# One more in-place DMA addition ahead of the third layer of a bias network

## The chip, the cores and the metric

The kernel runs on one core of one Trainium2 chip. The metric is the device time in microseconds (us) of one execution. In what follows PE is the matmul engine (TensorE), PEld its weight loads, DVE VectorE, ACT ScalarE, POOL GpSimd and SP SyncE, which here only issues DMAs.

## The reference

Four layers follow each other on an input of 2 x 512 x 32 x 32 floats. Only the first matters here, an attention whose keys are sampled at learned offsets and whose bias is a small network. For each of 8 groups of channels and each of 2 images (16 heads of the reference; the kernel handles two at a time, hence 8 pairs that it also calls groups, of 64 keys each):

```python
pos = grid_q[:, :, None, :] - grid_kv[:, None, :, :]       # 1024 queries x 64 keys x 2
bias = jnp.sign(pos) * jnp.log1p(jnp.abs(pos))
bias = jax.nn.relu(bias @ cpb_w1 + cpb_b1)                 # first layer: 128 hidden units
bias = jax.nn.relu(bias @ cpb_w2 + cpb_b2)                 # second layer: 128 hidden units
bias = (bias @ cpb_w3 + cpb_b3)                            # third layer: one number
sim = jnp.einsum('bhid,bhjd->bhij', qh, kh) + bias
attn = jax.nn.softmax(sim, axis=-1)
```

After it come a multilayer perceptron with a residual, a linear attention, a second attention and a gated output, all of which this change leaves as they are.

## The kernel before

All of it is one program in float32. The attention stage is one long loop over 512 keys (8 groups of 64), taken as 256 pairs `p` of keys. For each key the first layer is one DVE instruction, `first` (L353): it adds a row of `tab` for the key's column to one for its row and clips below at zero, and writes a tile `h` of 128 hidden units x 2048 (queries of two heads). `tab` is loaded by SP for 8 keys at a time (L161) and scaled by ACT (L173). There are 4 buffers for `h`.

The second layer, `second` (L619), takes the pair's two `h` tiles through a 128 x 128 weight matrix in four parts `o` of 32 output units. Each part is 8 matmuls of 128 x 32 by 512 columns, which go to the four column groups of the PE array (the trace has two records for each matmul, 16 for a part). ACT evicts each part with the bias and the Relu (L628) into tiles `r0` to `r3`; `hid` gives them 5, 1, 3 and 1 buffers. So the 32 partitions of one column group hold 32 hidden units of one (half of the queries, head), and four column groups are one tile.

The third layer is a weighted sum over the 128 hidden units. The weights' signs and sizes are folded into the second layer beforehand (`counted`, `placed`, `spread_out`), so that most of this sum is additions, of tiles and of neighbouring partitions:

- `combine` (L634, DVE) adds part 1 to part 0 and part 3 to part 2, with a ratio `rel`.
- `join` (L637) adds `r2` to `r0` by an accumulating DMA on POOL's queue, 512 KB.
- `fold` (L642) adds the odd partitions of `r0` to the even ones, an accumulating DMA on POOL's queue, 256 KB.
- `shift` (L649) copies every fourth partition to every fourth of a tile `xs`, on SP's queue, 128 KB; `d` shifts it, so that four pairs fill one `xs`.
- `meet` (L653) adds the other half of the folded partitions to it, on POOL's queue, 128 KB, and ends the life of `r0`.
- `third` (L664, PE) takes two `xs` tiles with 4 matmuls against the 33-column constant `cw3` into a PSUM tile `psim`; two such steps, with the constant shifted by a column, accumulate one `psim` of 32 keys.

What goes where in time is written out by hand. `at(n, when, fn, ...)` puts a call into a list for key `n` and for the even (0) or odd (1) parts of the second layer at that key; `run` calls them in that order, and `pin` keeps each engine's instructions in program order. So each engine, and each of the DMA queues of POOL and SP, works its list off in order, and an instruction that waits holds up all behind it on its engine. In the loop, `join(p - 1)` comes at key 2p, after part 1. The other transfers are given their keys by:

```python
at(2 * p + 4, 0, fold, p)
at(2 * p + 6, 0, shift, p)
at(2 * p + 7, 0, meet, p)
```

Beside the pairs run three plans of small steps, each placed by the same lists. `prepare(g)` samples a group's values and makes its keys and values (L685 to L760; `keys` and `values` write `kblk` and `vblk`, `weighted` by the output weights `wo` into `vwo`). `attend(g)` evicts `psim` (L791), transposes it onto the scores (`flip`, L803 and L816), and does the softmax (`top` L831, `sub` L835, `exp` L845, `total` L849, `inverse` L852, `norm` L856, `back` L862, `keep_` L871). `chain` computes the sampling offsets of the later groups (its taps are L230 on DVE), spread over keys 4 to 86 for groups 2 and 3 and 97 to 213 for groups 4 to 7.

After the loop the remaining transfers, the last third step and the last `attend` follow, without `pin`; beside them the scheduler places the output projection, 64 matmuls `po` (L1040), and the loads and sums of the first weights of the perceptron (L990, L1003, L973 to L983).

Of the kernel before, what the change touches and what calls it, by code (L numbers as in the profile page):

```python
# [10 lines left out]
F32 = mybir.dt.float32  # L11
AF = mybir.ActivationFunctionType
ALU = mybir.AluOpType
# [3 lines left out]
P = 128  # L17
B, C, H, W = 2, 512, 32, 32
# [39 lines left out]

_ORDER = [("same", P), ("below", P), ("place", P), ("rank", 1), ("third", 33)]
_CAT, _n = {}, 0  # L60
# [12 lines left out]
def conv_seq(  # L73
# [61 lines left out]
    with ExitStack() as ctx_l0:  # L135
# [11 lines left out]

        vwo = l0.tile([P, KC * B, C], F32, name="vwo")
        nc.gpsimd.memset(kblk, 0.0)
# [37 lines left out]
        def pin(ins):  # L187
            return tc.keep_in_program_order(ins) if started else ins
# [150 lines left out]
        sb3 = l0.tile([P, 4, 2], F32, name="sb3")  # L339
        cw3 = l0.tile([P, 33], F32, name="cw3")  # L340
        rel = l0.tile([P, 2], F32, name="rel")
# [23 lines left out]
        with tc.tile_pool(name="a", bufs=1) as a, tc.tile_pool(name="aps", bufs=3, space=PSUM) as aps, tc.tile_pool(  # L365
# [96 lines left out]
            def counted():  # L462
                pin(ve.tensor_copy(od[:, 7:9], pcnt))
                pin(ve.tensor_scalar(cpbw, cpbw, maj, None, ALU.mult))


                pin(ve.tensor_scalar(maj, total, 8.0, None, ALU.is_ge))
                pin(ve.tensor_scalar(t0, maj, -1.0, 1.0, ALU.mult, ALU.add))
                pin(ve.tensor_scalar(t1, total, -1.0, 16.0, ALU.mult, ALU.add))
                pin(ve.scalar_tensor_tensor(t0, t1, t0, below, ALU.mult, ALU.add))  # L470
                pin(ve.tensor_tensor(t1, oc("rank"), below, ALU.subtract))
                pin(ve.scalar_tensor_tensor(neg, total, maj, t1, ALU.mult, ALU.add))
                pin(ve.tensor_tensor(t0, t0, neg, ALU.subtract))
                pin(ve.scalar_tensor_tensor(t1, t0, pos, neg, ALU.mult, ALU.add))
                pin(ve.scalar_tensor_tensor(perm, oc("place"), t1, oc("same"), ALU.is_equal, ALU.mult))
# [119 lines left out]


        with tc.tile_pool(name="hid", bufs=3) as hid, tc.tile_pool(name="sm", bufs=1) as sm, tc.tile_pool(name="hps", bufs=2, space=PSUM) as hps, tc.tile_pool(
            name="sps", bufs=1, space=PSUM
# [13 lines left out]
            def second(p, o):  # L612

                ph = hps.tile([P, 2, 512], F32, name="ph")
                for i in range(2):
                    for t in range(4):
# [9 lines left out]
                        )  # L626
                r = hid.tile([P, 2, 512], F32, name=f"r{o}", bufs=(5, 1, 3, 1)[o])
                pin(nc.scalar.activation(r, ph, AF.Relu, bias=sb3[:, o, 1:2]))  # L628
# [9 lines left out]

            def fold(p):

                r = rs[p, 0]
                pin(nc.gpsimd.dma_start(r[0::2], r[1::2], accum_op=ALU.add))  # L642

            def shift(p):

                t, d = divmod(p, 4)
                if d == 0:
                    xs_[t] = hid.tile([P, 2, 512], F32, name="xs", bufs=3)
                pin(nc.sync.dma_start(xs_[t][d::4], rs[p, 0][0::4]))  # L649

            def meet(p):
                t, d = divmod(p, 4)
                pin(nc.gpsimd.dma_start(xs_[t][d::4], rs.pop((p, 0))[2::4], accum_op=ALU.add))  # L653

            def third(g, u):
                kb, i = divmod(u, 2)
                if i == 0:
                    psims[g, kb] = sps.tile([P, 512], F32, name=f"psim{kb}")
                for a in range(2):
                    xs = xs_.pop(g * J // 8 + 2 * u + a)  # L660
                    for c in range(2):
                        m = 2 * c + a
                        pin(
                            nc.tensor.matmul(  # L664
                                psims[g, kb][m * 32 : (m + 1) * 32, :],
                                lhsT=cw3[:, 1 - i : 33 - i],
                                rhs=xs[:, c, :],
                                start=(i == 0),
                                stop=(i == 1),
                                skip_group_check=True,  # L670
                            )
                        )

            def prepare(g):

                k, b = divmod(g, B)
                st = {}
                n = J * (g - 1) + 32
                here = slice(CO_AT[k] * P + b * J, CO_AT[k] * P + (b + 1) * J)
# [50 lines left out]
                def ordered(to, of):  # L730

                    to, of = to.rearrange("p (c x i) -> p c x i", c=2, i=2), of.rearrange("p (i x c) -> p c x i", c=2, i=2)
                    return to, of

                def keys():
                    for h, kb in np.ndindex(2, 2):
                        hs, ks = slice(h * DH, (h + 1) * DH), slice(kb * 32, (kb + 1) * 32)
                        to, of = ordered(kblk[hs, g % 2, h, ks], st["pk"][hs, 0, ks])
                        pin(nc.scalar.activation(to, of, AF.Identity, scale=DH**-0.5))

                def values():
                    for h, kb in np.ndindex(2, 2):
                        hs, ks = slice(h * DH, (h + 1) * DH), slice(kb * 32, (kb + 1) * 32)
                        to, of = ordered(vblk[hs, g % 2, h, ks], st["pk"][hs, 1, ks])
                        pin(nc.vector.tensor_copy(to, of))
# [13 lines left out]
                def weights():  # L759
                    pin(nc.scalar.copy(vwo[:, g, :], st["pw"]))  # L760

# [140 lines left out]
            for g in range(NG):  # L902
                prepare(g)
                for u in range(4):
                    at(J * g + 16 * u + 24, 0, third, g, u)
                if g < NG - 1:
                    attend(g, J * (g + 1) + 9, True)
            for p in range(NK // 2):
                at(2 * p + 4, 0, fold, p)
                at(2 * p + 6, 0, shift, p)  # L910
                at(2 * p + 7, 0, meet, p)

# [15 lines left out]

            chain(1, 2, 86, 82)
            chain(2, 4, 213, 116)  # L930

# [103 lines left out]
        for t in range(NT // 512):  # L1035
            ts_ = slice(t * 512, (t + 1) * 512)
            for o in range(KC):
                po = mh.tile([P, 512], F32, name="po")
                for k in range(KC):
                    nc.tensor.matmul(  # L1040
                        po,
                        lhsT=vwo[:, k * B + t // 2, o * P : (o + 1) * P],
                        rhs=q[:, k, ts_],
                        start=(k == 0),
                        stop=(k == KC - 1),
                    )
# [838 lines left out]
def _layout(a):  # L1885
# [50 lines left out]

    rank = p // 32 * 4 + p % 4
    same = p[:, None] % 32 // 4 == p[None] % 32 // 4
    put("same", same.astype(f), order)
    put("below", (same & (rank[:, None] < rank[None])).astype(f), order)  # L1940
    put("place", (np.array([0, 2, 1, 3])[p // 32] * 4 + p % 4).astype(f)[None], order)
    put("rank", rank.astype(f)[:, None], order)

    put("third", (np.arange(33)[None] == (1 + 8 * (p // 32) + 2 * (p % 4))[:, None]).astype(f), order)
    put("npy", -(4 * np.arange(8)[None] + p[:, None] // 32).astype(f))
# [56 lines left out]
```

## Time and profile before

| what | us |
|---|---|
| median of 3 runs (2698.12 to 2698.23) | 2698.2 |
| the profiled execution | 2697.67 |
| its span, from the first to the last instruction | 2695.9 |
| PE busy in the span | 2653.6 (98%) |
| DVE busy in the span | 2251.3 (84%) |
| ACT busy in the span | 1538.4 (57%) |
| POOL busy in the span | 669.8 (25%) |
| attention stage, first to last second-layer matmul | 44.0 to 1900.5 |

The page describes one execution. It gives, for each group of like instructions, the line and engine, what is written and read, the shape and the count; then, after the bar, the busy time in us and the mean ns of one; then the engine's idle time just before them and what ended it. Busy times of single instructions overlap at their ends: the trace has 2291 ns for a `first`, while the next instruction on DVE starts 2200 ns after it. So sums of durations are a little too long, and starts are used where it matters.

### The profile page before, as it was taken

How to read it: one execution, taken by the hardware profiler on the slowest of the kernel's cores; microseconds unless marked ns; L12 is line 12 of the kernel's file. 1: busy time of each engine (PE TensorE's matmuls, PEld its weight loads, DVE VectorE, ACT ScalarE, POOL GpSimd, SP SyncE). 2: the span in 40 equal slices, each digit the busy share in tenths (PEclk: the TensorE clock that was granted, in tenths of full speed). 3: DMA queues.
4: the chain of work that ended last, by engine and by line, in shares of the span. 5: the costliest groups of instructions: out<-in, count | busy, mean ns of one | idle time of the engine just before them, and what ended most of it. 6: DMA issues, size and time to landing. Idle time of an engine off the chain costs nothing.

```text
span 2695.9 us, 48423 instructions
## 1 busy us (share of the span) xinstructions
PE 2653.6 (98%) x19574; PEld 967.3 (36%) x19574; DVE 2251.3 (84%) x2009; ACT 1538.4 (57%) x1920; POOL 669.8 (25%) x784
## 2 busy tenths in 40 slices
PE   8999999999999999999999999999999999999997
PEld 4223323232332323333333333333444444455544
DVE  6999999999999999999999999999554445525646
ACT  7676677777667777866877776776221111001334
POOL 0333333333333333333333333333100000000001
PEclk9999999999999999999999999999999999999998
DMA  4777877877777787787788788787400000100001
GB/s 129 165 165 162 168 158 161 169 157 162 163 166 158 165 170 157 165 168 161 162 195 173 154 179 188 163 174 159 94 30 24 16 24 24 62 17 1 1 0 63
DMA packets 109327, 335.04 MB, mean 124 GB/s; under 512 B 18576, under 2 KB 28304, under 8 KB 108336
## 3 DMA queue, kind: packets, MB, share of 16 engines
q0 software_dynamic: 69632, 234.93, 46.7%
q1 hardware_dynamic: 38896, 96.51, 10.4%
q8 instruction: 154, 2.52, 0.4%
q14 instruction: 69, 0.57, 0.1%
q10 hardware_dynamic: 576, 0.51, 0.1%
HBM read 58.99 MB, written 4.46 MB: 24 GB/s over the span
## 4 chain that ended last, share of the span: by engine, by line
PE 81%; DVE 9%; issue 6%; ACT 2%; DMA 1%; POOL 1%; DVEq 0%; ACTq 0%; POOLq 0%
PE ph L619 51%; DVE h L353 4%; PE A L1105 4%; PE D L1105 4%; PE C L1105 4%; DVE r L634 3%; PE B L1105 2%; PE po L1040 2%; PE pg L1248 1%; PE pa L1359 1%; PE pu L1282 1%; PE psim L664 1%; PE pscore L1491 1%; DMA xs<-r 1%; PE pt L1511 1%
## 5 line engine op out<-in xcount | busy, mean ns | idle before, releaser
L619 PE MATMUL ph<-h,w2a 128*32 128x512 f32 x16384 | 1779.1, 593 | 6.0 <-ACT r L628 3.3
L628 ACT ACTIVATE r<-ph,sb 128x1024 f32<-128x1024 f32 x1024 | 1141.1, 1114 | 510.5 <-PE ph L619 487.3
L353 DVE CUSTOM_DVE_ANT_1 h<-tab 128x2048 f32<-128x2048 f32 x512 | 1172.9, 2291 | 13.0 <-PE ph L619 10.0
L619 PEld LDWEIGHTS ph<-h,w2a 128*32 128x32 f32 x16384 | 520.2, 109 | 1226.6 <-issue 801.7
L634 DVE SCALAR_TENSOR_TENSOR r<-r,rel,r 128x1024 f32<-128x1024 f32 x512 | 658.0, 1285 | 16.4 <-ACT r L628 15.8
L642 POOL DMA_DIRECT2D r<-r x256 | 219.5, 857 | 961.2 <-DMA r<-r 936.1
L637 POOL DMA_DIRECT2D r<-r x256 | 245.2, 958 | 280.4 <-DVE r L634 243.6
L653 POOL DMA_DIRECT2D xs<-r x256 | 306.6, 1198 | 12.2 <-issue 6.1
L173 ACT ACTIVATE tab<-tab,vec 128x256 f32<-128x256 f32 x252 | 136.9, 543 | 0.0
L1293 POOL MEMSET M<- 128x512 f32 x2 | 1.0, 524 | 435.3 <-DVE x L1169 435.3
L1145 ACT COPY u<-A 128x512 f32<-128x512 f32 x16 | 9.4, 585 | 146.9 <-PE A L1105 146.9
L1776 POOL TENSOR_TENSOR x<-x,aff 128x512 f32<-128x512 f32 x7 | 7.0, 1031 | 329.0 <-ACT e L1741 329.0
L1124 ACT ACTIVATE h<-h,vec 128x512 f32<-128x512 f32 x32 | 23.1, 721 | 113.7 <-DVE h L1127 113.7
L1127 DVE TENSOR_TENSOR h<-C,u 128x512 f32<-128x512 f32 x32 | 22.1, 691 | 48.2 <-PE C L1105 47.9
L1105 PE MATMUL A<-xn,w 128*128 128x512 f32 x128 | 60.3, 593 | 0.8 <-DVE x L1047 0.8
L1105 PE MATMUL C<-hT,w 128*128 128x512 f32 x128 | 60.3, 592 | 0.0
L1105 PE MATMUL A<-h,w 128*128 128x512 f32 x128 | 60.1, 592 | 0.0
L1040 PE MATMUL po<-q,vwo 128*128 128x512 f32 x128 | 56.3, 594 | 0.0
L230 DVE SCALAR_TENSOR_TENSOR acc<-q,vec,acc 128x128 f32<-128x128 f32 (+3 forms) x88 | 46.2, 525 | 0.8
L1165 DVE TENSOR_TENSOR x<-D,x 128x512 f32<-128x512 f32 x32 | 22.1, 691 | 25.8 <-PE D L1105 25.7
L856 ACT ACTIVATE e<-e,den 128x64 f32<-128x64 f32 x128 | 41.8, 338 | 1.9 <-DVE den L852 1.9
L1165 DVE TENSOR_TENSOR x<-C,x 128x512 f32<-128x512 f32 x32 | 22.1, 690 | 24.8 <-PE C L1105 24.8
(365 smaller groups left out, 1867.6 us busy)
## 6 DMA issues: line engine op xcount, KB each, us to landing
r<-r POOLq DMA_DIRECT2D x256, 512.0 KB, 5.2
r<-r POOLq DMA_DIRECT2D x256, 256.0 KB, 3.4
xs<-r SPq DMA_DIRECT2D x256, 128.0 KB, 3.9
xs<-r POOLq DMA_DIRECT2D x256, 128.0 KB, 5.6
tab<-fd SPq DMA_DIRECT2D x63, 512.0 KB, 5.6
lw<-in_l_w_dram SPq DMA_DIRECT2D x5, 1024.0 KB, 9.0
x<-in_x_dram SPq DMA_DIRECT2D x4, 1024.0 KB, 10.5
w<-in_mlp_w_dram SPq DMA_DIRECT2D x8, 512.0 KB, 4.3
```

Source lines behind the costliest of these rows:

```text
L173: return nc.scalar.activation(tf, tf if src is None else src[:, :, ax, :], AF.Identity, bias=0.0 if ax == 0 else v("L0_conv_cpb_b1"), scal ...
L230: pin(nc.vector.scalar_tensor_tensor(dst, src, wt_, dst, ALU.mult, ALU.add))
L353: nc.vector._custom_dve(TENSOR_ADD_SAT, out=h1, in0=columns.unsqueeze(1).to_broadcast([P, 32, 2, 32]), in1=rows_.unsqueeze(3).to_broadcast ...
L619: nc.tensor.matmul(ph[t * 32 : (t + 1) * 32, i, :], lhsT=w2a[:, o], rhs=h1s[2 * p + i][:, half * 16 : (half + 1) * 16, h, :], start=True, ...
L628: pin(nc.scalar.activation(r, ph, AF.Relu, bias=sb3[:, o, 1:2]))
L634: pin(nc.vector.scalar_tensor_tensor(r0, r1, rel[:, i : i + 1], r0, ALU.mult, ALU.add))
L637: pin(nc.gpsimd.dma_start(rs[p, 0], rs.pop((p, 2)), accum_op=ALU.add))
L642: pin(nc.gpsimd.dma_start(r[0::2], r[1::2], accum_op=ALU.add))
L653: pin(nc.gpsimd.dma_start(xs_[t][d::4], rs.pop((p, 0))[2::4], accum_op=ALU.add))
L1040: nc.tensor.matmul(po, lhsT=vwo[:, k * B + t // 2, o * P : (o + 1) * P], rhs=q[:, k, ts_], start=(k == 0), stop=(k == KC - 1),)
L1105: nc.tensor.matmul(banks[bank], lhsT=a[an][k], rhs=b_[bn_][k], start=(i < 4 and k == 0), stop=(k == n - 1), skip_group_check=True,)
L1165: nc.vector.tensor_tensor(to, t, to, ALU.add)
```

## The change

The partitions of the second layer are placed so that 8 neighbours, not 4, belong to one sum. A second `fold` with a stride of 2 adds every fourth partition's neighbour (64 partitions become 32, 128 KB), so `shift` and `meet` move 16 partitions (64 KB each) and 8 pairs fill one `xs`. A `psim` of 32 keys then needs one third step of 4 matmuls with a 32-column constant, and no accumulation. There are 8 third-layer matmuls per group where there were 16. `r0` gets 7 buffers. `vwo` is halved: the values of the second image are written over `wo`. `keys` and `values` become one instruction per head. The plans of `prepare`, `attend` and `chain` come 4 keys later. The core of the diff:

```diff
-        vwo = l0.tile([P, KC * B, C], F32, name="vwo")
+        vwo = l0.tile([P, KC, C], F32, name="vwo")
...
-                pin(ve.tensor_scalar(maj, total, 8.0, None, ALU.is_ge))
+                pin(ve.tensor_scalar(maj, total, 16.0, None, ALU.is_ge))
...
-                r = hid.tile([P, 2, 512], F32, name=f"r{o}", bufs=(5, 1, 3, 1)[o])
+                r = hid.tile([P, 2, 512], F32, name=f"r{o}", bufs=(7, 1, 3, 1)[o])
...
-            def fold(p):
+            def fold(p, step):
 
                 r = rs[p, 0]
-                pin(nc.gpsimd.dma_start(r[0::2], r[1::2], accum_op=ALU.add))
+                pin(nc.gpsimd.dma_start(r[0 :: 2 * step], r[step :: 2 * step], accum_op=ALU.add))
 
             def shift(p):
 
-                t, d = divmod(p, 4)
+                t, d = divmod(p, 8)
                 if d == 0:
                     xs_[t] = hid.tile([P, 2, 512], F32, name="xs", bufs=3)
-                pin(nc.sync.dma_start(xs_[t][d::4], rs[p, 0][0::4]))
+                pin(nc.sync.dma_start(xs_[t][d::8], rs[p, 0][0::8]))
 
             def meet(p):
-                t, d = divmod(p, 4)
-                pin(nc.gpsimd.dma_start(xs_[t][d::4], rs.pop((p, 0))[2::4], accum_op=ALU.add))
+                t, d = divmod(p, 8)
+                pin(nc.gpsimd.dma_start(xs_[t][d::8], rs.pop((p, 0))[4::8], accum_op=ALU.add))
...
-            def third(g, u):
-                kb, i = divmod(u, 2)
-                if i == 0:
-                    psims[g, kb] = sps.tile([P, 512], F32, name=f"psim{kb}")
+            def third(g, kb):
+                psims[g, kb] = sps.tile([P, 512], F32, name=f"psim{kb}")
                 for a in range(2):
-                    xs = xs_.pop(g * J // 8 + 2 * u + a)
+                    xs = xs_.pop(g * J // 16 + 2 * kb + a)
...
-                                lhsT=cw3[:, 1 - i : 33 - i],
+                                lhsT=cw3,
                                 rhs=xs[:, c, :],
-                                start=(i == 0),
-                                stop=(i == 1),
+                                start=True,
+                                stop=True,
...
-                n = J * (g - 1) + 32
+                n = J * (g - 1) + 36
...
-                    pin(nc.scalar.copy(vwo[:, g, :], st["pw"]))
+                    pin(nc.scalar.copy((vwo, wo)[b][:, k, :], st["pw"]))
...
-                for u in range(4):
-                    at(J * g + 16 * u + 24, 0, third, g, u)
+                for kb in range(2):
+                    at(J * g + 32 * kb + 43, 1, third, g, kb)
                 if g < NG - 1:
-                    attend(g, J * (g + 1) + 9, True)
+                    attend(g, J * (g + 1) + 13, True)
             for p in range(NK // 2):
-                at(2 * p + 4, 0, fold, p)
-                at(2 * p + 6, 0, shift, p)
-                at(2 * p + 7, 0, meet, p)
+                at(2 * p + 5, 1, fold, p, 1)
+                at(2 * p + 7, 0, fold, p, 2)
+                at(2 * p + 8, 1, shift, p)
+                at(2 * p + 10, 0, meet, p)
...
-            chain(1, 2, 86, 82)
-            chain(2, 4, 213, 116)
+            chain(1, 2, 90, 86)
+            chain(2, 4, 217, 116)
```

More of the change, by code (lines that the diff above doesn't have):

```diff
@@ L57 @@
 _CONSTS = [("ident", P), ("grid", 2 * J), ("gridf", J), ("npx", 1), ("npy", 8), ("sel3", 2)]
-_ORDER = [("same", P), ("below", P), ("place", P), ("rank", 1), ("third", 33)]
+_ORDER = [("same", P), ("below", P), ("place", P), ("rank", 1), ("third", 32)]
 _CAT, _n = {}, 0
@@ L339, in conv_seq @@
         sb3 = l0.tile([P, 4, 2], F32, name="sb3")
-        cw3 = l0.tile([P, 33], F32, name="cw3")
+        cw3 = l0.tile([P, 32], F32, name="cw3")
         rel = l0.tile([P, 2], F32, name="rel")
@@ L464, in counted @@
                 pin(ve.tensor_scalar(cpbw, cpbw, maj, None, ALU.mult))
-                pin(ve.tensor_scalar(maj, total, 8.0, None, ALU.is_ge))
+                pin(ve.tensor_scalar(maj, total, 16.0, None, ALU.is_ge))
                 pin(ve.tensor_scalar(t0, maj, -1.0, 1.0, ALU.mult, ALU.add))
-                pin(ve.tensor_scalar(t1, total, -1.0, 16.0, ALU.mult, ALU.add))
+                pin(ve.tensor_scalar(t1, total, -1.0, 32.0, ALU.mult, ALU.add))
                 pin(ve.scalar_tensor_tensor(t0, t1, t0, below, ALU.mult, ALU.add))
@@ L730, in ordered @@
                 def ordered(to, of):
-                    to, of = to.rearrange("p (c x i) -> p c x i", c=2, i=2), of.rearrange("p (i x c) -> p c x i", c=2, i=2)
+                    to, of = to.rearrange("p (k c x) -> p k c x", k=2, c=2), of.rearrange("p (k x c) -> p k c x", k=2, c=2)
                     return to, of
                 def keys():
-                    for h, kb in np.ndindex(2, 2):
-                        hs, ks = slice(h * DH, (h + 1) * DH), slice(kb * 32, (kb + 1) * 32)
-                        to, of = ordered(kblk[hs, g % 2, h, ks], st["pk"][hs, 0, ks])
+                    for h in range(2):
+                        hs = slice(h * DH, (h + 1) * DH)
+                        to, of = ordered(kblk[hs, g % 2, h, :], st["pk"][hs, 0, :])
                         pin(nc.scalar.activation(to, of, AF.Identity, scale=DH**-0.5))
                 def values():
-                    for h, kb in np.ndindex(2, 2):
-                        hs, ks = slice(h * DH, (h + 1) * DH), slice(kb * 32, (kb + 1) * 32)
-                        to, of = ordered(vblk[hs, g % 2, h, ks], st["pk"][hs, 1, ks])
+                    for h in range(2):
+                        hs = slice(h * DH, (h + 1) * DH)
+                        to, of = ordered(vblk[hs, g % 2, h, :], st["pk"][hs, 1, :])
                         pin(nc.vector.tensor_copy(to, of))
@@ L1041, in conv_seq @@
                         po,
-                        lhsT=vwo[:, k * B + t // 2, o * P : (o + 1) * P],
+                        lhsT=(vwo, wo)[t // 2][:, k, o * P : (o + 1) * P],
                         rhs=q[:, k, ts_],
@@ L1934, in _layout @@
     put("sel3", (p[:, None] % 32 == np.array([1, 2])[None]).astype(f))
-    rank = p // 32 * 4 + p % 4
-    same = p[:, None] % 32 // 4 == p[None] % 32 // 4
+    rank = p // 32 * 8 + p % 8
+    same = p[:, None] % 32 // 8 == p[None] % 32 // 8
     put("same", same.astype(f), order)
     put("below", (same & (rank[:, None] < rank[None])).astype(f), order)
-    put("place", (np.array([0, 2, 1, 3])[p // 32] * 4 + p % 4).astype(f)[None], order)
+    put("place", (np.array([0, 2, 1, 3])[p // 32] * 8 + p % 8).astype(f)[None], order)
     put("rank", rank.astype(f)[:, None], order)
-    put("third", (np.arange(33)[None] == (1 + 8 * (p // 32) + 2 * (p % 4))[:, None]).astype(f), order)
+    put("third", (np.arange(32)[None] == (8 * (p // 32) + p % 8)[:, None]).astype(f), order)
     put("npy", -(4 * np.arange(8)[None] + p[:, None] // 32).astype(f))
```

## The prediction

> **What bounds the kernel now.** I read the page's groups first, then stretches of the span, then the timeline, then the waits. The groups show two engines with nearly the same load in the attention stage (44 to 1901 us):
>
> ```profile
> L619 PE MATMUL ph<-h,w2a 128*32 128x512 f32 x16384 | 1779.1, 593 | 6.0 <-ACT r L628 3.3
> L353 DVE CUSTOM_DVE_ANT_1 h<-tab 128x2048 f32<-128x2048 f32 x512 | 1172.9, 2291 | 13.0 <-PE ph L619 10.0
> L634 DVE SCALAR_TENSOR_TENSOR r<-r,rel,r 128x1024 f32<-128x1024 f32 x512 | 658.0, 1285 | 16.4 <-ACT r L628 15.8
> ```
>
> PE spends 1779.1 us on the second layer; DVE spends 1172.9 + 658.0 = 1830.9 us building first layers and combining. A share over the stage can't say which ends last, so I cut it in two with the busy times by stretch (columns: stretch, length, busy PE, PEld, DVE, ACT, POOL, then PE clock, DMA share, GB/s):
>
> ```profile
> 118.00:800.00 682.00, 677.60 (x6281) 207.79 (x6277) 680.47 (x482) 490.76 (x574) 239.94 (x280) 1.00 0.79 164
> 865.00:1900.50 1035.50, 1034.96 (x9644) 321.68 (x9638) 1003.20 (x631) 752.23 (x889) 371.83 (x432) 1.00 0.80 168
> ```
>
> From 118 to 800 us DVE is idle for 1.53 of 682 us: **DVE bounds it**, because the offset networks of the later groups put their taps (L230) there. From 865 us PE is idle for 0.54 us and DVE for 32: **PE bounds it**. The timeline shows what a third-layer step costs where PE bounds:
>
> ```profile
> 1414.23 1.92 PE L619 MATMUL ph<-h,w2a 128*32 128x512 f32 x16
> 1415.98 1.04 PE L664 MATMUL psim<-xs,cw 128*32 128x512 f32 x8
> 1416.83 8.75 PE L619 MATMUL ph<-h,w2a 128*32 128x512 f32 x78
> ```
>
> Start to start, the step (4 matmuls, 8 records) takes 1416.83 - 1415.98 = 0.85 us. From the starts of the ph records, a plain pair of keys takes 6.87 us there and a pair with a step 7.73, so 0.86 us. Last, the waits:
>
> ```profile
> POOL r L642 <- DMA r<-r: 936.1, 250, 9.0
> POOL r L637 <- DVE r L634: 243.6, 138, 54.2
> ```
>
> POOL waits, 250 times and 936 us in all, for a join to land before it issues the fold, and another 244 us for DVE's combine. That is slack and not work: POOL is 25% busy over the span.
>
> **What the Trainium skill says.** "DMA: Bandwidth & Descriptors", section "SWDGE vs HWDGE vs iDMA": accumulation in a DMA is for GpSimd's queue alone. So the added fold cannot leave POOL; the trace has all its accumulating transfers there. The same page, "Two DMAs through the same engine are not ordered": the issuer must wait for the first transfer's semaphore before a dependent one. The 936 us above are that wait. "SBUF — State Buffer", "SBUF: two separate sides": VectorE with two SBUF inputs and GpSimd share a port pair. Partly seen: from one combine's start to the next DVE instruction is 1196 ns in the median, and about 1260 in 35 of the 71 combines that overlap a join's or a meet's issue; h keeps 2200 ns under POOL's issues.
>
> **The change, part by part.**
>
> *Third layer.* 4 steps a group become 2, 32 become 16, and each step of the new program still has 4 matmuls. By place (before): 12 steps from 118 to 800 us, 1 near 832, 18 from 865 on, 1 in the tail. In the new program, counted by the same pairs, 9 lie in the PE-bound part and 1 in the tail. PE-bound: 9 fewer x 0.858 = **-7.7 us**. In the DVE-bound part PE's relief brings only what DVE loses to waits, at most 1.53 us; I take half, -0.8, ends 0 and -1.5.
>
> *values and keys.* 4 copies of 64x32 become 2 of 64x64, on DVE and on ACT. On DVE the four take 0.55 us from start to start; I take 0.35 for two (estimate), so -0.2 a group. It counts only where DVE bounds, 3 groups: -0.6. ACT has 27% of a group free, and the four took 0.73 us: nothing. Sum of the DVE-bound part: **-1.4 us**.
>
> *The added fold.* 256 more issues on POOL. Rows L642 and L637 give 0.86 and 0.96 us each, 0.54 to 0.56 from start to start: POOL goes from about 36% to 47% of the stage. Per pair the accumulated bytes go from 896 to 960 KB, the copied ones on SP from 128 to 64. Records of 4096 bytes take 347 ns accumulating and 188 copying, so engine time per pair rises by 16 x 347 - 16 x 188 = 2.5 us over 16 engines, 0.16 us of 6.87: the DMA share goes from 0.80 to about 0.82. Nothing on the path while third and the buffers are in time. They are, by this reckoning: the join of pair p is issued some 2.8 us into key 2p+2, its landing is 5.2 (median), and the new order on POOL is join(p-1), second fold(p-3), first fold(p-2), meet(p-4). Each fold waits for a transfer issued a whole pair (6.87 us) earlier, where the fold waited for the join right ahead of it. The join's 5.2 us and the fold's 3.4 fit into 6.87. The last meet before a step should land near key 2p+11, and the step stands at the end of key 2p+13: 10 us of slack. r0 gets 7 buffers instead of 5 for a life 3 keys longer, so one key more slack. What is queued behind a late fold: the next meet and join on POOL, then ACT's evictions into r2 (3 buffers); on SP, behind a late shift, the load of tab. A late landing (10.8 us for the worst join) is absorbed as now.
>
> *Contention.* The burst on POOL is one issue longer and now begins right behind a combine, so its last issue, the meet, reaches into the next combine, 2.2 us later. Ends: 0, and 64 ns on each of 2 combines a pair. In the DVE-bound part (682 us, some 100 pairs) I take 10 ns a pair (9 in 100 combines are slow now): **+1.0 us**.
>
> *Steps moved by four keys* (prepare, attend, chain). Their DVE work is the same, but the third step that stood at pair 12 of a group is gone, and it was there that PE let DVE catch up. I measured DVE's lead as the end of the h of an odd key to the first matmul that reads it: 2.64 us at rest in group 5, least 0.91 at pair 14. Taking 0.86 away leaves 0.05, which is what the trace shows where PE does wait. So the edge is just reached: 0 to 0.4 us in each of three groups, I take **+0.6 us**. ACT's and PE's own moved work stays beside what it had.
>
> *r0, vwo, cw3.* r0 takes 8 KB a partition more, vwo 8 KB less; batch 1 writes wo over after the matmul that makes the value: the copy waited for that matmul already. The constant is one column shorter. Nothing.
>
> *The tail.* One more transfer in a row after the last key: landing 3.4 and issue 0.8, about 4.2 us later. The cover is the output projection (po, L1040): the old order has 19 of its matmuls ahead of the last two third matmuls, the new one 29, that is 25 us from 1901.8. The chain join, fold, fold, shift, meet ends near 1903.3 + 18.7 = 1922, before 1926.7. Left behind it are 24 po matmuls, 20.6 us, over attention's end and the first weight sums, which waited for it; in the trace they were done 20 us before PE needed them, and they move by 8.6. Nothing; with the cover gone, +4.
>
> Sum: -7.7 - 1.4 + 1.0 + 0.6 = -7.5. The profiled execution took 2697.67 us (span 2695.9); the median, 2698.2, is 0.5 above it and takes the same difference: 2690.7, rounded **2690.5 us**.
>
> **Rivals.**
>
> *PE bounds everywhere.* If DVE's lack of idle time before 800 us were only followed from PE, all 16 steps go: 16 x 0.858 = 13.7, 2684.5 us. For it: PE is 677.6 of 682 us busy there. Against: h starts back to back (2200 ns apart from the combine), and PE waits with a lead of 0.05 us at some twenty pairs.
>
> *Given back.* Contention of 30 ns on each of 2 combines over the 100 DVE-bound pairs (6.0 us) and the lead's edge (3 x 0.4 = 1.2) against the -9.1 of the steps and copies: -1.9, 2696.3 us; with half of it, 2693. For it: half of the overlapping combines are slow now. Against: most overlaps are short.
>
> *Slower: POOL's issues stretch both combines of each pair.* Place: L634 on DVE, by 64 ns: 100 pairs x 2 x 0.064 = 12.8 in the DVE-bound part, and pairs 9 to 16 of groups 4 to 7, where the lead is short, 4 x 8 x 2 x 0.064 = 4.1. Without my 1.0 and 0.6: -9.1 + 16.9 = +7.8, 2706 us. It decides from about half the combines on (9.1 us of stretch). For it: the shared port and the measured 64 ns. Against: h, longer and with more overlap, shows none of it.
>
> *The change does not do what it says,* in that third waits for late transfers on PE: one wait of 1 us a step would cost 16. The 10 us of slack speak against it; the worst landing now (10.8) says that one or two steps could be touched.
>
> **How the numbers follow.** Likeliest case 0.58, its own range 2688 to 2693; PE everywhere 0.08; given back 0.24; slower (with a late third) 0.10. The range 2685.5 to 2698.5 leaves out the slower case and most of the fastest. A measurement of this kernel tells about 0.2% (5.4 us) from no change: faster 0.58 + 0.08 + 0.04 = 0.70, within 0.20, slower 0.10.
>
> **What would show it.** Right: in the PE-bound groups the time per group falls from 230.5 to about 228.8 us; in groups 1 to 3 together it falls by less than 2.5; POOL's wait for r<-r falls well below 936; no third matmul waits for xs. Wrong: L634's mean over 1285 by 30 ns or more, groups 1 to 3 each faster by 1.7, PE idle ahead of L664, or a gap between the po matmuls near 1927.

## The result, and the profile after

The changed kernel takes 2689.24 us in the median (2687.59 to 2689.72, 6 runs) where the one before takes 2698.03 beside it (2696.46 to 2698.23, 6 runs): a ratio of 0.9968, interval 0.9956 to 0.998, so 8.8 us faster. The profiled execution took 2689.26 us with a span of 2687.2. Executions of either kernel differ by up to 2.5 us, and in the profiled ones such differences lie in the stages after the attention; so causes are read below from the attention stage (first to last second-layer matmul). It went from 1855.96 us to 1846.46, by 9.5 us.

The page's groups after (columns: line, engine, operation, out<-in, shape, count; after the bar busy us and mean ns of one; then idle time before them and what ended most of it):

```profile
L621 PE MATMUL ph<-h,w2a 128*32 128x512 f32 x16384 | 1777.6, 593 | 8.7 <-ACT r L630 4.0
L354 DVE CUSTOM_DVE_ANT_1 h<-tab 128x2048 f32<-128x2048 f32 x512 | 1174.3, 2294 | 11.5 <-PE ph L621 9.3
L636 DVE SCALAR_TENSOR_TENSOR r<-r,rel,r 128x1024 f32<-128x1024 f32 x512 | 659.5, 1288 | 13.3 <-ACT r L630 12.8
L644 POOL DMA_DIRECT2D r<-r x512 | 472.2, 1136 | 200.8 <-DMA r<-r 189.6
L639 POOL DMA_DIRECT2D r<-r x256 | 236.4, 923 | 730.8 <-DVE r L636 674.1
```

Nothing on PE or DVE got shorter or longer by more than a few ns: a `first` is 2294 ns (2291 before) and a `combine` 1288 (1285). What changed is the last column of POOL's rows. The two folds (L644, now 512 issues) wait for transfers 189.6 us, not 936.1, and POOL's idle time is now mostly ended by DVE's `combine` (674.1 us, not 243.6). POOL waits for its source, and much less for its own transfers. What these take, from the page's DMA issues after (count, KB each, median us from issue to landing):

```profile
r<-r POOLq DMA_DIRECT2D x256, 512.0 KB, 5.0
r<-r POOLq DMA_DIRECT2D x256, 256.0 KB, 5.9
r<-r POOLq DMA_DIRECT2D x256, 128.0 KB, 4.7
...
xs<-r POOLq DMA_DIRECT2D x256, 64.0 KB, 5.5
```

The join and the meet land about as before (5.2 and 5.6), and the first fold later (3.4 before). Each has a turn of 6.87 us to land in; the experiments below ask whether that is what hides them.

The same stretches as before, the second one ended where the stage now ends (length, busy PE, PEld, DVE, ACT, POOL, PE clock, DMA share, GB/s):

```profile
118.00:800.00 682.00, 675.58 (x6248) 206.10 (x6244) 681.16 (x475) 491.67 (x569) 320.37 (x375) 1.00 0.85 164
865.00:1891.00 1026.00, 1024.30 (x9538) 317.92 (x9532) 1000.40 (x625) 752.35 (x887) 489.86 (x575) 1.00 0.87 170
```

In the first, DVE's idle time fell from 1.53 us to 0.84, so DVE is still nearly full there; e1 and e2 below show in which groups that is a bound. In the second PE still bounds. The length of each group of 64 keys, from the starts of its second-layer matmuls, tells where the 9.5 us came from (the last column is the stage; kernels of the experiments below are in the same table):

| kernel | g0 | g1 | g2 | g3 | g4 | g5 | g6 | g7 | stage |
|---|---|---|---|---|---|---|---|---|---|
| before | 231.1 | 235.3 | 234.2 | 236.2 | 231.2 | 230.5 | 230.5 | 226.9 | 1856.0 |
| after | 230.1 | 234.1 | 233.9 | 235.9 | 229.5 | 228.8 | 228.8 | 225.3 | 1846.5 |
| e1 before, few taps | 228.8 | 235.3 | 231.2 | 235.6 | 231.2 | 230.5 | 230.5 | 226.9 | 1850.0 |
| e2 after, few taps | 226.9 | 234.1 | 229.5 | 235.1 | 229.5 | 228.8 | 228.8 | 225.3 | 1838.0 |
| e4 third twice | 230.1 | 235.9 | 235.1 | 237.0 | 231.3 | 230.6 | 230.6 | 227.0 | 1857.5 |
| e8 taps on POOL | 234.2 | 237.3 | 244.1 | 241.1 | 229.5 | 230.1 | 229.5 | 225.3 | 1871.0 |
| e9 fold before join | 230.1 | 234.6 | 245.6 | 240.9 | 239.3 | 249.1 | 247.1 | 243.9 | 1930.7 |
| e10 second behind first | 245.0 | 264.5 | 261.4 | 263.2 | 264.6 | 265.2 | 266.8 | 260.3 | 2091.0 |
| e11 e9 without tab loads | 230.1 | 233.5 | 233.8 | 235.5 | 229.4 | 228.7 | 228.7 | 227.1 | 1847.0 |

Groups 4 to 7 lost 1.6 to 1.7 us each, two third steps; groups 1 to 3 lost 1.8 together and group 0 lost 1.0. Up to pair 22 of group 3 the new kernel is 1.83 us ahead, and from there to the end it gains 7.66.

The tail, from the timeline after (start, length, engine, line, what; in brackets the idle time before it):

```profile
1898.67 19.05 PE L1041 MATMUL po<-q,vwo 128*128 128x512 f32 x44
...
1911.39 0.75 POOL L655 DMA_DIRECT2D xs<-r  x1 [2.91 <-DMA xs<-r]
...
1917.65 1.05 PE L664 MATMUL psim<-xs,cw 128*32 128x512 f32 x4
1918.63 1.12 PE L1041 MATMUL po<-q,vwo 128*128 128x512 f32 x2
```

The last `meet` is issued at 1911.39 and the last third step runs at 1917.65 straight behind the output projection, with no gap. The last `meet` has landed at 1913.8 us, 3.9 us ahead of that step. The chain that became one transfer longer is covered by the `po` matmuls.

### The profile page after: what moved, and what is told of

It is laid out like the page before. It is cut to its first block, busy times and chain, and to the rows that moved or that the text cites. A ratio compares the mean times of both kernels' runs of the same rounds, so it can differ in the third digit from the quotient of the medians.

```text
span 2687.2 us, 48166 instructions
## 1 busy us (share of the span) xinstructions
PE 2640.8 (98%) x19446; PEld 960.8 (36%) x19446; DVE 2248.8 (84%) x1993; ACT 1537.4 (57%) x1904; POOL 884.0 (33%) x1040
## 4 chain that ended last, share of the span: by engine, by line
PE 83%; DVE 10%; issue 4%; ACT 2%; DMA 1%; DVEq 0%; POOL 0%; ACTq 0%
PE ph L621 53%; DVE h L354 5%; PE A L1106 4%; PE D L1106 4%; PE C L1106 4%; DVE r L636 3%; PE po L1041 2%; PE B L1106 2%; PE pg L1249 1%; PE pa L1360 1%; PE pu L1283 1%; PE pscore L1492 1%; DMA r<-r 1%; PE pz L1521 1%; DVE acc L231 1%
## 5 line engine op out<-in xcount | busy, mean ns | idle before, releaser
L354 DVE CUSTOM_DVE_ANT_1 h<-tab 128x2048 f32<-128x2048 f32 x512 | 1174.3, 2294 | 11.5 <-PE ph L621 9.3
L636 DVE SCALAR_TENSOR_TENSOR r<-r,rel,r 128x1024 f32<-128x1024 f32 x512 | 659.5, 1288 | 13.3 <-ACT r L630 12.8
L644 POOL DMA_DIRECT2D r<-r x512 | 472.2, 1136 | 200.8 <-DMA r<-r 189.6
L639 POOL DMA_DIRECT2D r<-r x256 | 236.4, 923 | 730.8 <-DVE r L636 674.1
L655 POOL DMA_DIRECT2D xs<-r x256 | 319.1, 1247 | 105.2 <-DMA xs<-r 90.1
L1249 PE MATMUL pg<-xt 128*128 128x512 f32 (+3 forms) x128 | 36.4, 439 | 1.4 <-ACT xt L1247 1.1
```

The costliest lines, as they stand in the source:

```text
L354: nc.vector._custom_dve(TENSOR_ADD_SAT, out=h1, in0=columns.unsqueeze(1).to_broadcast([P, 32, 2, 32]), in1=rows_.unsqueeze(3).to_broadcast ...
L636: pin(nc.vector.scalar_tensor_tensor(r0, r1, rel[:, i : i + 1], r0, ALU.mult, ALU.add))
L639: pin(nc.gpsimd.dma_start(rs[p, 0], rs.pop((p, 2)), accum_op=ALU.add))
L644: pin(nc.gpsimd.dma_start(r[0 :: 2 * step], r[step :: 2 * step], accum_op=ALU.add))
L655: pin(nc.gpsimd.dma_start(xs_[t][d::8], rs.pop((p, 0))[4::8], accum_op=ALU.add))
L1249: nc.tensor.matmul(pgs[i], lhsT=xt[:, i * P : (i + 1) * P], rhs=xt[:, i * P :], start=(t == 0), stop=(t == 7),)
```

## The experiments

My theory for all of them: a third step costs its 0.86 us where PE bounds and next to nothing where DVE bounds; the added transfer is hidden because POOL waits for nothing that was issued in the same turn. The rivals were that PE bounds everywhere, that POOL's issues stretch DVE, and that the wide spacing is not needed.

### e1 and e2: take DVE's taps away, from both kernels

```diff
                 for i, tap in enumerate(taps):
+                    if tap[1] != 1:
+                        continue
                     at(n - taken + i * taken // 36, 1, ch.tap, *tap)
```

> The kernel before with 30 of the 36 taps of the two later offset networks left out (so its sampling offsets are others). Theory (DVE bounds groups 0 to 3 only because of the taps): groups 1 to 3 come near the 230.5 us of groups 5 to 7 but keep the chain's own stalls; about 8 us (5 to 12) faster than before, 2690. Rival (PE bounds everywhere, taps are hidden): no change, within 2 us.

> The changed kernel with the same 30 of 36 taps left out (other sampling offsets). Theory: PE bounds all groups now, so all 16 removed third steps count: faster than the kernel before with few taps by 13.7 us (12 to 14.5), about 1.7 in each of the eight groups. Rival (what the change gains does not depend on DVE): the same 8.8 us as between the full kernels.

e1 took 2691.57 us in the median (2690.23 to 2692.37, 9 runs), ratio 0.9978 (0.9968 to 0.9987) to before; e2 2680.99 (2680.51 to 2681.28, 5 runs), ratio 0.9939 (0.9926 to 0.9951). So with DVE relieved the change is worth 10.6 us between the medians, and 12.0 in the stage (1850.0 to 1838.0), where with the taps it was worth 9.5. The table shows where: group 2 now loses 1.7 us by the change, like a PE-bound one, where it lost 0.3. That DVE's taps bound group 2, and that the steps there were free for that reason, is shown. For group 1 the same pair of runs says no: it takes 235.3 us before the change with and without the taps, and 234.1 after it, while DVE's idle time in it rises from 1.3 to 7.7 us (before the change) when the taps go. The full 13.7 us was missed: groups 1 and 3 kept 235 us in both kernels and gave 1.23 and 0.48. By the pairs' periods the rest lies in pairs where PE waits for the offset network itself (pair 12 of group 3 takes 8.49 us with a third step before the change, and pair 14 takes 8.47 without one after it), so there the step stood inside a wait. That reading is argued from the periods and was not tried by itself.

### e3: the added transfer alone

The kernel before, with one more accumulating DMA of the same size in each pair, on rows that nobody reads afterwards:

```diff
+            def again(p):
+                r = rs[p, 0]
+                pin(nc.gpsimd.dma_start(r[1::4], r[3::4], accum_op=ALU.add))
...
+                at(2 * p + 6, 0, again, p)
                 at(2 * p + 6, 0, shift, p)
```

> The kernel before with one more accumulating transfer a pair of the size of the second fold (32 partitions, 128 KB), between partitions that are no longer read; the third layer is as before. Theory (the transfer is hidden, its issue does not slow DVE): within 1.5 us of before, combines (L634) within 5 ns of 1285. Rival (issues on POOL stretch the combines): L634 up by 30 ns or more, 6 to 17 us slower. Second rival (POOL's in-order queue gets full in the old order, about 6.5 of 6.87 us a pair): slower by more than 20 us, with ACT waiting for DMAs.

It took 2698.73 us in the median (2696.32 to 2702.53, 13 runs), ratio 1.0006 (0.9998 to 1.0014). In the profiled execution the stage is 1856.08 us, 0.12 over before, and DVE's row does not move:

```profile
L634 DVE SCALAR_TENSOR_TENSOR r<-r,rel,r 128x1024 f32<-128x1024 f32 x512 | 657.5, 1284 | 16.5 <-ACT r L628 15.8
```

1284 ns against 1285. In that execution 256 more issues on POOL neither delay nor stretch anything; the slower rival of the prediction (64 ns on each combine) is out. The profiled execution (2696.32 us) is the fastest of the 13, though, and six of the others took 2699.7 to 2702.5 us, where no run of the kernel before took over 2698.43. What made those longer was not looked into; the median is 0.9 us over that of the kernel before.

### e4: put the third steps' time back

```diff
-                    for c in range(2):
+                    for c in (0, 1, 0, 1):
```

> The changed kernel with every third-layer matmul issued twice (same result): PE's load of before, all else as changed. Theory: groups 4 to 7 get back 1.7 us each, groups 0 to 3 together no more than 3, sum +8 to +10 over the changed kernel, about 2698. Rival (PE bounds everywhere): +13.7, about 2703.

It took 2701.98 us (2699.99 to 2702.43, 21 runs), ratio 1.0014 (1.0007 to 1.0021): 12.7 over the changed kernel in the median, 10.7 between the profiled executions and 11.1 in the stage. In groups 4 to 7 it gives back 1.77 to 1.79 us each, which confirms the price of a step. But group 1 pays 1.77 for its two doubled steps, group 2 1.16 and group 3 1.05, where I had most of it hidden, while group 0 hides it: 4.0 us in groups 0 to 3 where I had at most 3, and 11.1 in the stage where I had 8 to 10. So "DVE-bound" holds by pair and not by group: a third step that stands just ahead of the flips of `attend` meets a DVE that idles (2.5 us of idle time in group 1, 0.7 in the changed kernel), and there PE's time is on the path. That DVE had run to the end of its lead there is argued, not tried. And e4 is not simply the change without its saving: with as many third-layer matmuls as before, but in two double steps a group at other pairs, groups 1 to 3 are 2.2 us slower than before and group 0 is 1.0 faster.

### e5: one buffer of r0 less

```diff
-                r = hid.tile([P, 2, 512], F32, name=f"r{o}", bufs=(7, 1, 3, 1)[o])
+                r = hid.tile([P, 2, 512], F32, name=f"r{o}", bufs=(6, 1, 3, 1)[o])
```

> The changed kernel with 6 buffers of r0 instead of 7. Theory: r0 of pair p is written again in key 2p+12, and the meet that ends its life lands near key 2p+11, so ACT waits little or not at all: within 1.5 us of the changed kernel (2689). Rival (the seventh buffer is what keeps the longer line of transfers off the path): ACT's wait for DMAs (line 630) grows to 1 us or more a pair in many pairs, 20 us or more slower.

It took 2692.36 us (2689.07 to 2696.79, 17 runs), ratio 0.998 (0.9973 to 0.9987); the stage is 2.9 us longer than after. That is over the 1.5 us that I expected and far under the rival's 20. Nearly all of it lies in groups 5 and 6 (1.5 and 1.2), in one pair each: pair 29 of group 5 takes 9.52 us where it took 8.04. The `meet` that frees the buffer for that pair landed 3.6 us into it in group 5 and 3.3 in group 6, and held up the eviction. The seventh buffer is worth some 3 us; six would be enough but for a few landings.

### e6 and e7: the same transfers, closer

e6 puts each transfer closer behind the one it needs; e7 puts both folds in one turn, one right behind the other, and leaves `shift` and `meet`.

```diff
-                at(2 * p + 5, 1, fold, p, 1)
-                at(2 * p + 7, 0, fold, p, 2)
-                at(2 * p + 8, 1, shift, p)
-                at(2 * p + 10, 0, meet, p)
+                at(2 * p + 4, 0, fold, p, 1)     # e7: as e6
+                at(2 * p + 5, 0, fold, p, 2)     # e7: at 2 * p + 4
+                at(2 * p + 6, 1, shift, p)       # e7: as after
+                at(2 * p + 7, 1, meet, p)        # e7: as after
```

> The changed kernel with its transfers one to two keys behind the one each needs instead of one to three (folds at keys 2p+4 and 2p+5, shift 2p+6, meet 2p+7). On POOL's queue each second fold now stands one transfer behind the fold it needs. Theory: POOL waits for DMAs again (300 us or more in all, 190 in the changed kernel), but its round of join, fold, fold, meet stays under the 6.87 us of a pair: within 1.5 us of the changed kernel. Rival (the wider spacing is what hides the added transfer): more than 5 us slower.

> The changed kernel with both folds in the same key list (2p+4), so that POOL issues fold, fold, join with nothing between. Theory: POOL's queue then waits for a join (5.0 us) and a fold (3.4 to 5.9 us) one after the other in each pair, about 9.5 us for the 6.87 us that PE needs; 256 x 2.6 = some 670 us slower (500 to 900), ACT and PE waiting for r2. Rival (the queue does not matter, the transfers overlap anyway): within 20 us.

e6 took 2786.13 us (2777.29 to 2803.0, 6 runs), ratio 1.0333 (1.0311 to 1.0356): 97 us slower than the changed kernel, where my theory had 1.5. e7 took 3457.33 us (2 runs), ratio 1.2818 (1.2796 to 1.284), 768 slower, near what I expected. POOL's waits in e6 (total us, times, longest):

```profile
POOL r L644 <- DMA r<-r: 771.4, 401, 7.6
...
POOL r L639 <- DVE r L636: 70.3, 14, 54.7
```

The `join` waits for DVE only 14 times, 212 in the changed kernel: whenever DVE is done, POOL is still behind, held by a fold that waits for a landing. In e7 that goes on to ACT, whose evictions wait for joins, and so to PE:

```profile
ACT r L630 <- DMA r<-r: 768.6, 228, 7.6
```

768.6 us of waits, and 768 us of loss. So the schedule's spacing is what hides the transfer. But e6 changes three gaps at once, so one more pair of runs took two of them, those ahead of the two folds, one by one.

### e9 and e10: which gap

```diff
-                at(2 * p + 5, 1, fold, p, 1)
-                at(2 * p + 7, 0, fold, p, 2)
+                at(2 * p + 4, 0, fold, p, 1)     # e9 alone
+                at(2 * p + 6, 0, fold, p, 2)     # e10 alone
```

> The changed kernel with only the first fold earlier: ahead of the next join on POOL, which makes it wait for the join of the turn before. The second fold still comes a whole turn later. It asks which of the waits of the close schedule cost its 97 us. The round that this leaves in POOL's order is join, its landing (5.0 to 5.2 us in the median, 6.2 at 90%), first fold's issue (about 0.9), next join: 6.1 us in the median, under the 6.87 of a pair, so a slow landing can be made up at some 0.7 us a pair. My theory, that a round has to be shorter than the pair with the landings as they are: +0 to +30 us, likeliest +10, and POOL's wait ends by DVE in most pairs still. Rival, that any dependent transfer less than a pair behind its source costs what the close schedule cost, or half of it: +50 to +100 us.

> The changed kernel with only the second fold earlier: one transfer (the meet) behind the first fold in the same turn of POOL, so it waits for that fold's landing (5.9 us in the changed kernel, behind a join) before the next join can be issued. The round is join's issue, first fold, its landing, second fold, next join: some 0.55 + 5.9 + 0.9 = 7.3 us, over the 6.87 of a pair, so no lead can make it up. My theory: slower by about (7.3 - 6.87) x 250 pairs = +110 us over the changed kernel, between +40 and +160 since a fold with less in flight beside it lands sooner; the join's wait for DVE nearly vanishes. Rival, that the join's own wait chain (join, first fold, next join) was what cost in the close schedule: within 5 us of the changed kernel here, and the cost in the other run.

e9 took 2768.03 us (2760.67 to 2775.21, 4 runs), ratio 1.026 (1.0238 to 1.0283): 79 over the changed kernel, where my theory said at most 30. e10 took 2943.6 us (2942.18 to 2950.81, 4 runs), ratio 1.0917 (1.0899 to 1.0936): 254 over it, where it said 40 to 160. Both were missed, on the same side. e10's timeline shows its round:

```profile
1402.58 0.84 POOL L644 DMA_DIRECT2D r<-r  x1 [5.01 <-DMA r<-r]
1403.12 1.19 POOL L639 DMA_DIRECT2D r<-r  x1
1403.65 1.53 POOL L644 DMA_DIRECT2D r<-r  x1
1404.19 1.79 POOL L655 DMA_DIRECT2D xs<-r  x1
1411.22 0.84 POOL L644 DMA_DIRECT2D r<-r  x1 [5.25 <-DMA r<-r]
```

Second fold, join, first fold, meet are issued 0.54 us apart; then POOL waits until the first fold has landed, 7.0 us after the meet was issued. From join to join it is 8.12 us in the median and 8.20 in the mean; the changed kernel has 7.21. 0.99 us in 256 pairs is 253 us, about the whole loss: 244.5 us lie in the stage, and the rest behind it, where PE is idle for 8.5 us ahead of the last third step. The mechanism was right and the size was not: I had added 5.9 us for the landing and one issue to it, but behind a second fold and a join the first fold lands 6.7 us after its issue (median), which with 1.07 ahead of it and some 0.35 behind it makes 8.1.

In e9 the median round is 6.92 us, which alone would cost little, and the mean is 7.54. Sorted by the pair's number modulo 4, the mean intervals from one join to the next are 6.94, **9.33**, 7.17 and 6.92 us, and the joins land in the median after 5.9, **8.9**, 5.9 and 5.8 us. Every fourth pair SP loads `tab`. POOL's and SP's timelines there:

```profile
1409.67 0.87 POOL L644 DMA_DIRECT2D r<-r  x1 [1.72 <-DMA r<-r]
1410.22 1.22 POOL L639 DMA_DIRECT2D r<-r  x1
...
1419.43 0.87 POOL L644 DMA_DIRECT2D r<-r  x1 [4.54 <-DMA r<-r]
```

```profile
1410.74 0.51 SPq L162 DMA_DIRECT2D tab<-fd  x1
```

The join issued at 1410.22 has `tab`'s 512 KB issued 0.5 us behind it, and the fold that waits for it goes at 1419.43, 9.2 us later. In the whole of e9 the joins with the load at most 0.8 us behind them (44) land after 9.1 us in the median, and the five with the load 1.5 to 2.5 us behind after 5.0. The chain that ended last, by engine, turns over with it, from the changed kernel to e9:

```profile
PE 83%; DVE 10%; issue 4%; ACT 2%; DMA 1%; DVEq 0%; POOL 0%; ACTq 0%
```

```profile
DMA 55%; PE 32%; POOL 5%; issue 4%; DVE 3%; ACT 2%; DVEq 0%; ACTq 0%; POOLq 0%; SPq 0%
```

e6 has the same pattern: its joins beside the load land after 8.4 us and the others after 5.9. Its 97 us are thus likely to be mostly e9's 79; no run took the load out of e6. Of the 18.7 us between the spans of e6 and e9, 6.3 lie in the stage and 12.4 outside it, where in e6 PE is idle for 6.9 us ahead of the last third step, waiting for its `xs`.

### e11 and e12: the loads of tab left out

```diff
-                tabs[ch] = tab_load(ch)
+                tabs[ch] = tabs[ch - 2]
...
-            for ch in range(1, NK // TK):
+            for ch in range(1, 2):
```

> The schedule with the first fold ahead of the next join (79 us over the changed kernel), without tab's loads and their scaling after the first two: every later key reads one of the first two tab tiles again, so the first layer's values are other ones. In that schedule one join in four, the one beside tab's load on SP's queue, lands after 8.9 us in the median and the others after 5.8 to 5.9; the interval to the next join is 9.33 us there and 6.92 to 7.17 elsewhere. Theory: the cost is this one round in four, which the others, at about 6.8 us, have no reserve to make up. Then the fourth join lands like the others, the four intervals come to 6.9 to 7.2, and the kernel falls by 60 to 79 us to 2690 to 2710. Rival, that the wait of the first fold in front of the join costs by itself and tab's load only decides where it shows: it stays above 2740.

> The same leaving out of tab's loads and their scaling, from the changed kernel: the control. There the join beside the load lands 0.8 to 1 us later than the others (5.7 against 4.7 to 4.9 in the median) and POOL's order has a whole pair for it. Theory: no more than 3 us faster than the changed kernel (2686 to 2690), since the load is hidden there. Rival, that the load costs PE or DVE something by itself: 10 us or more faster.

e11 took 2688.81 us (2686.93 to 2690.86, 6 runs), ratio 0.9969 (0.9955 to 0.9983); e12 2687.64 (2685.91 to 2688.11, 5 runs), ratio 0.9966 (0.995 to 0.9981). So without the loads e9's schedule is as fast as the changed kernel (1.2 us over e12), and its 79 us came from the one late join in four, which the other rounds could not make up; while from the changed kernel the loads could be taken away for 1.6 us. The scaling on ACT went with the loads; that it is the load and not the scaling is read from the landings in e9, which follow the distance to the load. In e11 the joins of all four pairs land after 5.1 to 5.3 us, and the intervals are 7.18 to 7.33. POOL still waits for landings a great deal:

```profile
POOL r L644 <- DMA r<-r: 471.4, 243, 9.7
...
POOL r L639 <- DVE r L636: 224.9, 139, 54.5
```

243 of the 512 folds wait, 471 us in all, and it costs next to nothing: the join still waits for DVE 139 times, so POOL is back on time. In these runs a wait of POOL costs only when its round runs over the pair's 6.87 us and stays over. e9's three ordinary rounds have next to no reserve, so a fourth that is over by 2.4 us is never made up.

### e8: the later taps on POOL

The changed kernel with 6 buffers of `r0`, and the later groups' taps moved from DVE to POOL, each as two instructions:

```diff
+                    if self.k0:
+                        tmp = self.tile("tmp").rearrange("p (y x) -> p y x", x=SIDE)[:, :, xo]
+                        by = wt_.unsqueeze(2).to_broadcast(list(tmp.shape))
+                        pin(nc.gpsimd.tensor_tensor(tmp, src, by, ALU.mult))
+                        pin(nc.gpsimd.tensor_tensor(dst, dst, tmp, ALU.add))
+                        return
```

> The changed kernel with r0 in 6 buffers and the taps of the two later offset networks moved from DVE to POOL, each as a multiply and an add (two tensor_tensor there). Theory that DVE alone bounds groups 0 to 3: DVE is freed of about 33 us of taps and the time comes near that of the kernel with few taps, 2681 (8 us faster than the changed kernel). Rival (POOL's two-input operations take the port pair that DVE's two-input operations use): combines or first layers beside a POOL tap get longer by up to the tap's length, some 0.5 to 1 us, 66 taps: 10 us or more slower than the changed kernel, in groups 0 to 3 alone.

It took 2714.93 us (2711.97 to 2715.81, 5 runs), ratio 1.0065 (1.0052 to 1.0078): 26 slower than the changed kernel, although DVE has fewer instructions to do. The loss lies in groups 0 to 3, where the taps are, but for 2 us in groups 5 and 6 (as with the 6 buffers in e5). Late transfers behind the taps on POOL are not the cause: DVE does not wait for them, and is idle for 0.23 us from 118 to 800 us, against 0.84 in the changed kernel. The groups (as above):

```profile
L234 POOL TENSOR_TENSOR tmp<-q,vec 128x128 f32<-128x128 f32 (+3 forms) x66 | 128.0, 1940 | 0.0
L235 POOL TENSOR_TENSOR acc<-acc,tmp 128x128 f32<-128x128 f32 (+3 forms) x66 | 116.7, 1768 | 5.4
...
L642 DVE SCALAR_TENSOR_TENSOR r<-r,rel,r 128x1024 f32<-128x1024 f32 x512 | 685.0, 1338 | 14.3 <-ACT r L636 13.8
```

The combine's mean went from 1288 to 1338 ns. From start to next start, combines beside these POOL instructions take 1542 ns (86 of them) and others 1196; a `first` 2406 (117) against 2201. That is 29.7 and 23.8 us. "SBUF — State Buffer", section "SBUF: two separate sides", of the Trainium skill calls the port pair of VectorE and GpSimd an exclusive lock, on which the later instruction waits out the earlier. The timeline of this run agrees, in both directions:

```profile
563.13 2.84 DVE L360 CUSTOM_DVE_ANT_1 h<-tab 128x2048 f32<-128x2048 f32 x1
563.89 2.67 POOL L235 TENSOR_TENSOR acc<-acc,tmp 128x256 f32<-128x256 f32 x1
565.89 1.75 DVE L642 SCALAR_TENSOR_TENSOR r<-r,rel,r 128x1024 f32<-128x1024 f32 x1
```

The addition on POOL starts beside a `first` that ends at 565.97, and ends 0.59 us after it; all 21 additions of this size that start beside a `first` or a `combine` end 0.59 to 0.60 us after it. So the means of 1.8 and 1.9 us on POOL are mostly waiting. The `combine` that starts at 565.89, while the addition has 0.67 us to go, takes 0.48 us longer than its usual 1.27. Of 60 `first` that start while a tap runs on POOL, 56 are late by the rest of the tap less some 0.13 us (within 0.025 us); the 57 that start ahead of a tap and meet it only later lose nothing in the median. The 0.2 to 0.35 us that DVE loses on average is thus what is left of a short tap, and not a sign that both run side by side. POOL's issues of DMAs, of which e3 has 256 more, show no such addition. So here POOL's free time could take transfers, and not this arithmetic.

## Why the prediction was right

The predicted 2690.5 us is 1.3 over the median measured. The main terms and the reason for the hidden transfer hold; that the total came so near is in part luck: the stage gained 2.0 us more than the sum of -7.5, and the difference between executions outside the stage (0.8 us in the profiled pair) took some of it back. By its own steps:

- **PE-bound part**, -7.7 predicted: -7.66 measured from pair 22 of group 3 on. A step's price, 0.86 us, held, and e4 pays it again from the other side. Groups 5 and 6 went from 230.5 to 228.8 as named.
- **DVE-bound part**, -1.4: -1.83 measured up to there, with contention included. Of its two terms, DVE's idle time from 118 to 800 us fell by 0.7 us (0.8 taken), and the copies on DVE take some 0.49 us a group where they took 0.62, 0.13 less (0.2 taken). The bound by DVE's taps is shown by e2, where group 2 gives 1.7 us as soon as DVE has less to do; in group 1 it is refuted by e1 (235.3 us with and without the taps). So the prediction was too broad in taking the whole stretch as bounded by DVE because of the taps. What e4 adds: the part is a patchwork of pairs, and the two steps that it doubles in each of groups 1 to 3 cost 1.05 to 1.77 us there, against 1.7 for two at the full price.
- **Contention**, +1.0: nothing. Waits aside, combines keep their mean pitch, 1202 ns in both kernels; those over 1240 ns are 43 in both, and 44 in e3, which adds as many issues. This term was mis-sized, and is half of the 2 us by which the stage gained more than the sum.
- **The lead's edge**, +0.6: 0.03 us in each of groups 5 to 7, 0.08. The lead at pair 16 of groups 5 and 6 came out at 0.05 us, exactly as worked out, but a lead of 0.05 is still a lead: the edge was reached and hardly passed.
- **The added fold**, nothing: right in effect, and for the reason given: a transfer that the fold needs was issued a turn earlier (e9, e10). e11 adds that less than a whole turn is enough where no landing is late. Two numbers in that step were wrong. The slack between the last meet's landing and the third step was called 10 us; it is 3.5 to 8.2, median 5.4, to the wait on PE's queue that stands ahead of the step, and some 2 us more to its first matmul. The reckoning had the last meet landed one key (3.4 us) after the start of key 2p+10; it is issued 0.2 to 6.2 us after that and lands 4.8 to 8.7 us after it. And the DMA share rose to 0.85 and 0.87, not 0.82: over the stage from 0.789 to 0.852. The sum had the count of the 4096-byte packets right, which makes 0.02 of it, and took their times as fixed; but an accumulating one took 361 ns in the mean where it had taken 347, and a copying one 203 for 190, which makes 0.036. The 4,096 small packets that it left out (16 for each added transfer, about 21 ns each) make 0.003. Neither number reached the path.
- **r0**, nothing: right with 7 buffers, as far as the runs show. With 6 it would have been +3 (e5), so the "one key more slack" was not spare.
- **The tail**, nothing: right, the third step follows the projection without a gap, with 29 `po` matmuls ahead of it as counted and 3.9 us to spare.
- **PE bounds everywhere** (2684.5) is out by groups 1 to 3, which lost 1.8 us and not 5.1, and by e2; **given back** and the **slower rival** (POOL's issues stretch combines) are out by the rows L636 and by e3; a **late third** is out, since PE is never idle ahead of a third step.

The stage's 9.5 became 8.4 between the profiled executions: 0.8 was lost in the span outside it, and 0.3 outside the span. The span outside the stage is 837.9 to 840.6 us in the profiled executions, but for the 851 of e6, e7 and e10, whose queue is late at the end.

## What to carry to other kernels

Work taken off an engine is worth its time only in the pairs where that engine bounds: cut the stage by place before multiplying. In an in-order queue, add up the round from one issue through the landing it waits for to the same issue of the next turn, with the landing as it is behind the transfers in front of it and in its worst regular turn. In these runs waits cost next to nothing while the rounds could make up their worst turn within the period (e11), and the whole excess when they could not (e9, e10). A whole turn between dependent transfers buys this, and is paid for in buffers.

## What the runs showed of the hardware

- One join in four lands 3 us later (8.9 against 5.9 us) when a 512 KB load on another queue is issued 0.5 us behind it; with the load 2 us behind it, as in the changed kernel, it lands after 4.9 us and the next join after 5.7. The distance is not the whole of it: in e6, 14 joins with the load 1.5 to 2.5 us behind took 7.3. With the loads left out (e11) no join in four is late.
- How long a transfer took went with what was ahead of it in its queue: the 256 KB fold lands after 3.4 us in the kernel before, 3.7 in e6 where it is ahead of the join, 5.9 in the changed kernel where it is behind one and a fold, and 6.7 in e10.
- Two-input arithmetic on POOL and DVE's `first` and `combine` waited for each other in e8, the later for the rest of the earlier: 56 of 60 `first` that started while a tap ran on POOL were late by the rest of it less 0.13 us. On average a `first` beside a tap became 9% longer and a `combine` 29%. 256 more DMA issues on POOL (e3) left the combines at 1284 ns against 1285.
